# Two vectors held in PSUM, eight product tiles in a ring of six banks, and a new order in the first group

## The chip, the cores and the metric

The kernel runs on one core of one Trainium2 chip. The metric is the device time of one execution in microseconds (us). Engines are named as the profile names them: PE multiplies matrices (PEld is its weight load), DVE, ACT and POOL work element by element, SP only issues transfers. ACT and POOL issue transfers too; ACTq, SPq and POOLq are these queues.

## The reference, cut to what matters

Two graph layers, each with a residual and a layer norm, over 4096 nodes with 512 features. The change lies in the first layer, at its beginning:

```python
support = (inputs @ weight).reshape(N, H, D).transpose(1, 0, 2)       # N=4096, H=4, D=128
f1 = jnp.einsum('hnd,hdo->hn', support, weight_u)[:, None, :]
f2 = jnp.einsum('hnd,hdo->hn', support, weight_v)[:, :, None]
logits = f1 + f2
w = jnp.where(logits >= 0, logits, SLOPE * logits)
masked = w * adjacency[None]
mask = masked != 0
attn = jax.nn.softmax(jnp.where(mask, masked, NEG), axis=-1) * mask
out = jnp.einsum('hij,hjd->hid', attn, support)
out = out.transpose(1, 0, 2).reshape(N, H * D) + bias + inputs @ proj_w + proj_b
x = _layernorm(x + out)
```

The second layer is a masked attention with eight heads over the same adjacency, then a projection, a residual and a layer norm. All is float32. The change doesn't touch it.

## The kernel before, in words

**Stages.** The first stage computes x @ weight ("s", the support), x @ proj_w + x + biases ("b", the base) and the two dots of every support row and head with weight_u and weight_v. Then comes the first layer's aggregation: 4 windows of 1024 rows x 4 heads x 32 tiles of 128 nodes. After it come the second layer's projections and its attention.

**The first stage's groups.** The nodes are taken in eight groups of 512 (the loop over `g`, L900). A group multiplies its 512 x 512 block of x by two 512 x 512 weights, each by a scheme of seven products of half-size blocks in place of eight (Strassen-like, with sums of blocks of x and of the weights made beforehand). So a group has 14 products: numbers 1 to 7 for "s" and for "b"; the text writes s1, b1, s5 and so on. `product` (L831) does one: 4 float32 matmuls (the profile has 8 records for them), and then what follows on the other engines. Products 1, 5, 6 and 7 open a PSUM tile. Product 2 accumulates into the tile of 1, 3 into that of 5, 4 into that of 7, each after the first content has been read.

**What follows a product.** Products 1 and 5 are copied out by ACT (L862) and 2 too (L864). Product 6 is added by DVE (L866). Product 7 is added by DVE (L868), and POOL adds a further term (L870). Products 3 and 4 are added by DVE (L873); for b, POOL then adds the biases (L877) and SP stores the base (L879).

**The dots.** `dots(g, s4, n, m)` (L807) does 8 of the 32 dots of a group for a quarter of the support block: a DVE multiplication of a 128x128 slice of the support with a slice of `uv`, with a sum along the row (L813). `uv` (L644) holds both vectors on all partitions in SBUF. A dictionary `todo` (L903) says after which product each quarter is done. `factors` (L677), one group later, makes exponentials on ACT, scales the support on POOL (L696) and stores it.

**x.** `load_x` loads a group's x from SP, `turn_x` transposes it on DVE (four pieces a group, L736), and `combine_x` makes the four sums: 0 and 1 on DVE (L793, L795), 2 and 3 on POOL (L797, L800). Both run a group ahead.

**Weights.** The two weights come in column halves m and row halves c, in pieces of 64 KB: half 0 on ACT's queue, half 1 on SP's (`load_w0`, L657). `combine_w` (L759) makes sums of weight blocks: those of s on DVE, those of b on POOL. Before that POOL adds the identity into proj_w, 32 x 32 at a time (L889).

**PSUM.** Of the eight banks six form the ring `op` (tiles "o_ps"), in which a new tile waits until the one six before it has been read. The pool `xp` (tiles "x_ps") has the other two. Before the change products 7 live in `xp`; later in the kernel `xp` serves to transpose the first layer's result.

**Order.** The order of instructions on each engine is the order of the program text: nothing rearranges it. `Later` (L32 on) only puts calls off by a number of steps. The lambdas in `beside` (L718 on) put other work beside the products of given groups: the narrowing of the adjacency to bfloat16 (POOL's queue), its transposition (SP's queue), its shrinking to fp8 (ACT, L601), and in the last group the first three steps of the aggregation's front (`front`, L621: a sign on ACT, L628; a mask on DVE, L632; a weighting on DVE, L637). The aggregation's matmuls are L1055; they use tiles of the ring `op`.

## Time and profile before

| what | value |
|---|---|
| median of 3 runs | 3367.14 us (3366.89 to 3367.37) |
| the profiled execution's own time | 3365.75 us |
| its span, first to last instruction | 3364.0 us |
| PE busy | 3325.7 us (99% of the span) |
| DVE busy | 2423.3 us (72%) |
| POOL busy | 2227.4 us (66%) |
| ACT busy | 1986.5 us (59%) |
| 256 dots (L813) | 125.1 us on DVE, 549 ns mean |
| first product's start, first matmul of the aggregation | 7.66 us, 215.69 us |

A line of the timeline reads: start in us from the span's beginning, length in us, engine, line of the kernel, operation, output <- inputs with their shapes, count; in brackets how long the engine had been idle and what released it. Lengths of PE instructions are modelled, their starts are recorded, so distances between starts are used. A line of the page's list of groups reads: line, engine, operation, names and shapes, count | busy us, mean ns of one | idle time before, and what ended it.

### The profile page before, as it was taken

To read this page: it belongs to the slowest core of one execution; us is meant where nothing else is said; L and a number is where in the kernel's file an instruction comes from. 1 tells how busy PE (TensorE), PEld (TensorE's weight loads), DVE (VectorE), ACT (ScalarE), POOL (GpSimd) and SP (SyncE) were. 2 spreads that over 40 slices of the span, in tenths; PEclk is the share of its full clock that TensorE was granted. 3 is DMA by queue.
4 is the path that set the end of the run, shared out by engine and by line. 5 is a ranking of instruction groups with operands and counts; after the bars stand their busy time and mean duration, and the time that the engine had idled before them with its cause. 6 is when DMAs were issued, how large, how long until landed. Compare 5 with 4: busy or idle time off the path is not lost.

```text
span 3364.0 us, 66621 instructions
## 1 busy us (share of the span) xinstructions
PE 3325.7 (99%) x27050; PEld 1950.4 (58%) x27050; DVE 2423.3 (72%) x2892; ACT 1986.5 (59%) x2461; POOL 2227.4 (66%) x1590
## 2 busy tenths in 40 slices
PE   8999999999999999999999999999999999999998
PEld 7889999999999855643333333333333333333333
DVE  7999998898998711167776667666676766667676
ACT  1257877878876421156655656566566656656554
POOL 5641030040030365579999999999999999999996
PEclk9999999999999999999999999999999999999999
DMA  7968869679441443378889888989988889798884
GB/s 167 228 165 172 219 171 214 148 180 199 142 121 64 112 152 113 140 205 205 200 204 220 223 209 190 212 196 241 211 189 212 191 207 252 186 210 191 208 197 111
DMA packets 400335, 620.41 MB, mean 184 GB/s; under 512 B 166929, under 2 KB 249873, under 8 KB 398993
## 3 DMA queue, kind: packets, MB, share of 16 engines
q0 software_dynamic: 97520, 258.77, 42.1%
q1 hardware_dynamic: 300544, 354.92, 34.5%
q8 instruction: 215, 3.52, 0.4%
q10 hardware_dynamic: 1952, 2.36, 0.3%
q14 instruction: 104, 0.84, 0.1%
HBM read 315.87 MB, written 117.64 MB: 129 GB/s over the span
## 4 chain that ended last, share of the span: by engine, by line
PE 86%; DVE 6%; POOL 3%; DMA 3%; issue 1%; ACT 0%; SPq 0%; ACTq 0%; POOLq 0%; DVEq 0%
PE o_ps L1055 26%; PE o_ps L1368 24%; PE s_ps L1106 23%; PE s_ps L1171 5%; DVE prod L813 3%; PE s_ps L1432 3%; PE s_ps L1164 3%; POOL q_sum L1343 2%; DMA p<-p 2%; PE o_ps L845 1%; POOL p L1353 1%; PE s_ps L1387 1%; DVE p L637 0%; PE x_ps L1036 0%; DVE xT L736 0%
## 5 line engine op out<-in xcount | busy, mean ns | idle before, releaser
L1343 POOL TENSOR_TENSOR q_sum<-q_sum,p 128x1024 f32<-128x1024 f32 x538 | 1374.5, 2555 | 66.6 <-DMA p<-p 37.1
L1323 DVE TENSOR_TENSOR p<-s_ps,adjT 128x1024 f32<-128x1024 f32 x896 | 1044.8, 1216 | 467.6 <-ACT s_ps L1320 428.1
L1320 ACT ACTIVATE s_ps<-s_ps 128x1024 f32<-128x1024 f32 x1021 | 967.2, 1007 | 598.1 <-PE s_ps L1106 595.5
L1106 PE MATMUL s_ps<-q_sb,k_sb 64*64 64x512 f32 x8192 | 943.5, 589 | 3.0 <-DVE p L1323 3.0
L1368 PE MATMUL o_ps<-p,v_sb 64*64 64x512 f32 x8192 | 943.6, 590 | 0.0
L1055 PE MATMUL o_ps<-sup_t,p 128*128 128x129 f32 x8192 | 922.5, 275 | 4.6 <-DVE p L637 4.5
L1055 PEld LDWEIGHTS o_ps<-sup_t,p 128*128 128x128 f32 x8192 | 919.9, 192 | 5.3 <-DVE p L637 5.2
L637 DVE SCALAR_TENSOR_TENSOR p<-fr_t,dj,az 128x1024 f32<-128x1024 f32 x512 | 656.0, 1291 | 79.4 <-PE o_ps L1055 52.0
L1106 PEld LDWEIGHTS s_ps<-q_sb,k_sb 64*64 64x64 f32 x8192 | 312.2, 133 | 570.3 <-issue 451.5
L1368 PEld LDWEIGHTS o_ps<-p,v_sb 64*64 64x64 f32 x8192 | 310.3, 133 | 570.6 <-issue 560.6
L628 ACT ACTIVATE z<-fr_t,f 128x1024 fp8e4<-128x1024 f32 x512 | 558.3, 1145 | 119.2 <-DVE az L632 118.8
L1353 POOL DMA_DIRECT2D p<-p x412 | 438.0, 1302 | 10.2 <-PE o_ps L1368 8.6
L1019 POOL DMA_DIRECT2D agg<-base_d x32 | 28.7, 1206 | 516.0 <-ACT agg L1005 515.8
L1323 DVE TENSOR_TENSOR p<-s_ps,md 128x1024 f32<-128x1024 f32 x128 | 150.9, 1217 | 68.3 <-ACT s_ps L1320 62.1
L632 DVE TENSOR_TENSOR az<-adjT,z 128x512 int32<-128x512 int32 x256 | 175.6, 686 | 4.0 <-ACT z L628 3.4
L588 POOL COPY seen<-token 128x1 f32<-128x1 f32 x24 | 14.5, 606 | 245.9 <-DVE token L586 245.9
L1178 ACT ACTIVATE sb<-s_ps 128x1024 f32<-128x1024 f32 x35 | 35.8, 1023 | 191.9 <-PE s_ps L1171 129.1
L601 ACT ACTIVATE adjT<-stage 128x1024 fp8e4<-128x1024 bf16 x128 | 130.6, 1051 | 6.4 <-DMA stage<-adj_d 6.4
L1193 POOL TENSOR_TENSOR sb<-sb,sb 128x1024 f32<-128x1024 f32 x36 | 84.9, 2374 | 72.1 <-ACT sb L1178 72.1
L813 DVE CUSTOM_DVE_ANT_0 prod<-s,uv 128x128 f32<-128x128 f32 x256 | 125.1, 549 | 5.1 <-DMA uv<-in_L_gnn_weight_u_dram 2.6
L1217 DVE COPY k_sb<-s_ps 128x1024 f32<-128x1024 f32 x12 | 14.7, 1225 | 140.7 <-PE s_ps L1171 91.0
L1432 PE MATMUL s_ps<-wo_sb,on 128*128 128x512 f32 x240 | 110.8, 604 | 0.0
(187 smaller groups left out, 2176.5 us busy)
## 6 DMA issues: line engine op xcount, KB each, us to landing
p<-p POOLq DMA_DIRECT2D x412, 512.0 KB, 9.1
k_sb<-k_d SPq DMA_DIRECT2D x128, 512.0 KB
v_sb<-v_d SPq DMA_DIRECT2D x128, 512.0 KB
adj_d<-in_adj_dram POOLq DMA_DIRECT2D x32, 1024.0 KB, 10.9
sup_t<-sup_d SPq DMA_DIRECT2D x120, 258.0 KB
fr_t<-fr_d SPq DMA_DIRECT2D x16, 1024.0 KB
adjT_d<-adjT SPq DMA_DIRECT2D x32, 512.0 KB
adjT<-adjT_d SPq DMA_DIRECT2D x32, 512.0 KB
```

Of the source, the lines that this page charges most:

```text
L628: nc.scalar.activation(z[:, k, :], fr[:, 0, :], AF.Sign, bias=fs[j // GT][:, 0, (j + k) % GT, h:h + 1], saturate=False)
L632: nc.vector.tensor_tensor(az.bitcast(I32), adjT[w, j // CJ][:, j % CJ:j % CJ + 2, :].bitcast(I32), z.bitcast(I32), op=ALU.bitwise_and)
L637: nc.vector.scalar_tensor_tensor(p, fr[:, 1, :], dj[j // GT][:, j % GT, h:h + 1], az_t[w, h, j // 2][:, j % 2, :], op0=ALU.max, op1=ALU.mult)
L813: nc.vector.tensor_tensor_reduce(prod, s4[:, h, t, 0:D0], uv[:, k, h * D0:(h + 1) * D0], 1.0, 0.0, op0=ALU.mult, op1=ALU.add, accum_out=fs ...
L1055: nc.tensor.matmul(o[t // BK][:, t % BK, :], p[:, t * P:(t + 1) * P], s, start=(j == 0 and t % BK == 0), stop=(j == NT - 1), skip_group_ch ...
L1106: nc.tensor.matmul(s[c:c + MS, e, :], k[r, a + c:a + c + MS], qt[g, m][r, :], start=True, stop=True)
L1320: nc.scalar.activation(s, s, AF.Exp)
L1323: nc.vector.tensor_tensor(p, s, keep[:, None, :].to_broadcast([P, HP, G]), op=ALU.mult)
L1343: nc.gpsimd.tensor_tensor(q, q, p, op=ALU.add)
L1353: later.at(2, lambda: nc.gpsimd.dma_start(a, b, accum_op=ALU.add))
L1368: nc.tensor.matmul(o[c, n, :], v[r, j % CH, c], p[r, e, :], start=(j == 0), stop=(j == NT - 1))
L1432: nc.tensor.matmul(s, on_t[g][:, m, t * P:(t + 1) * P], wo_sb[:, m, :], start=(m == 0), stop=(m == NP1 - 1))
```

## The change

It has four parts. First, `uv` is copied by ACT into two PSUM tiles of `xp` before the first group, and the dots read these. Second, products 7 take their tiles from the ring `op`, so that eight tiles a group pass through six banks. Third, the first group has an order of its own for the 14 products (`begin`); the dots are placed by product rather than by position (in the later groups at the same places as before), and the first group's `turn_x` and `combine_x` for the next group come later. Fourth, on SP's queue the second half of weight comes ahead of the second half of proj_w, and POOL adds the identity to that half of proj_w after the sums of x; the weights' sums are regrouped.

```diff
-            for m, queue in ((0, nc.scalar), (1, nc.sync)):
+            for queue, m, srcs in ((nc.scalar, 0, ((w_sb, weight), (pw_sb, proj_w))),
+                                   (nc.sync, 1, ((w_sb, weight),)),
+                                   (nc.sync, 1, ((pw_sb, proj_w),))):
                 for c in range(2):
-                    for dst, src in ((w_sb, weight), (pw_sb, proj_w)):
+                    for dst, src in srcs:
                         load_w0(queue, dst, src, c, m)
...
-                                prod, s4[:, h, t, 0:D0], uv[:, k, h * D0:(h + 1) * D0], 1.0, 0.0,
+                                prod, s4[:, h, t, 0:D0], uv_ps[k][:, h, :], 1.0, 0.0,
...
-                if i in (1, 5, 6):
+                if i in (1, 5, 6, 7):
                     tiles[kind, i] = op.tile([P, G], F32, name="o_ps")
-                elif i == 7:
-                    tiles[kind, i] = xp.tile([P, GT, P], F32, name="x_ps").rearrange(
-                        "p t r -> p (t r)")
...
-            for m in range(2):
+            def add_identity(m):
...
+            add_identity(0)
             combine_x(0, 0)
             combine_w(nc.vector, "s", (5,))
-            combine_x(0, 1)
+            for i in (1, 2, 3):
+                combine_x(0, i)
             combine_w(nc.vector, "s", (6, 7, 4))
-            combine_w(nc.gpsimd, "b", (5, 6))
-            combine_x(0, 2)
-            combine_w(nc.gpsimd, "b", (7, 4))
-            combine_x(0, 3)
+            add_identity(1)
+            combine_w(nc.gpsimd, "b", (5, 6, 7, 4))
             nc.gpsimd.dma_start(bb, on_all_partitions(proj_b, D), accum_op=ALU.add)
-            kinds = ("s", "b")
+            uv_ps = [xp.tile([P, H0, D0], F32, name="x_ps") for _ in range(2)]
+            for k in range(2):
+                nc.scalar.activation(uv_ps[k], uv[:, k, :].rearrange("p (h d) -> p h d", h=H0),
+                                     AF.Copy)
+            usual = [(kind, i) for i in (1, 5, 2, 6, 7, 3, 4) for kind in ("s", "b")]
+            begin = [("s", 1), ("b", 1), ("s", 2), ("b", 2), ("s", 5), ("s", 6), ("s", 7),
+                     ("b", 5), ("s", 3), ("b", 6), ("s", 4), ("b", 7), ("b", 3), ("b", 4)]
             for g in range(NG):
...
-                todo = {5: lambda: dots(g, s4, 0, 0), 10: lambda: dots(g, s4, 0, 1),
-                        11: lambda: dots(g, s4, 1, 1), 12: lambda: dots(g, s4, 1, 0)}
-                plan = (1, 5, 2, 6, 7, 3, 4) if g else (1, 2, 5, 6, 7, 3, 4)
-                for k, (i, kind) in enumerate((i, kind) for i in plan for kind in kinds):
+                plan = usual if g else begin
+                todo = {}
+                for i, wait, n, m in ((2, 1, 0, 0), (3, 0, 0, 1), (7, 3, 1, 1), (4, 0, 1, 0)):
+                    todo.setdefault(plan.index(("s", i)) + wait, []).append((n, m))
+                for k, (kind, i) in enumerate(plan):
...
-                    if k in todo:
-                        todo[k]()
-                    first = 0 if g else 7
+                    for nm in todo.get(k, ()):
+                        dots(g, s4, *nm)
+                    first = 0 if g else 10
                     if g + 1 < NG and first <= k < first + KC:
                         turn_x(g + 1, k - first)
-                    first = 6 if g else 10
-                    if g + 1 < NG and first <= k < first + 4:
-                        combine_x(g + 1, k - first)
+                    if g + 1 < NG and (6 <= k < 10 if g else k == 13):
+                        for n in (k - 6,) if g else range(4):
+                            combine_x(g + 1, n)
```

## The prediction

> **What bounds the kernel now.** Measurement can tell about 0.2% (6.7 us) of this kernel from no change. The page says PE is busy 99% of the span, so only time in which PE waits can be won, and any new PE wait is paid. The change lies in the first stage (0 to about 226 us), so I read PE there in order of time: eight groups of 14 products, 8 matmul records each.

> ```profile
> 17.18 1.89 PE L845 MATMUL o_ps<-fr_t,p 128*128 128x256 f32 x8
> 23.26 5.26 PE L845 MATMUL o_ps<-fr_t,p 128*128 128x256 f32 x16 [4.20 <-POOL fr_t L759]
> 28.36 1.89 PE L845 MATMUL o_ps<-more_w,p 128*128 128x256 f32 x8
> 40.45 1.89 PE L845 MATMUL o_ps<-w_sb,xT 128*128 128x256 f32 x8
> 64.62 1.89 PE L845 MATMUL o_ps<-w_sb,xT 128*128 128x256 f32 x8
> ...
> 185.91 1.89 PE L845 MATMUL o_ps<-w_sb,xT 128*128 128x256 f32 x8
> ...
> 210.44 3.53 PE L845 MATMUL x_ps<-fr_t,xT 128*128 128x256 f32 x8 [3.65 <-DVE s L868]
> 215.69 5.52 PE L1055 MATMUL o_ps<-sup_t,p 128*128 128x129 f32 x48
> 225.53 26.30 PE L1055 MATMUL o_ps<-sup_t,p 128*128 128x129 f32 x208 [4.32 <-DVE p L637]
> ```

> Group 1 starts at 40.45, group 2 at 64.62: 24.17 us, which is 14 products of 1.727. PE is packed there. From group 1 to group 7 (185.91) it takes 145.46 us for 6 x 24.178 = 145.07: only 0.4 us is lost in the steady part. PE loses 4.2 us in group 0 and 3.65 + 4.32 us at the end, each followed by about 1.6 us of slow matmuls (two products from 23.26 take 5.10 us, not 3.45). At the end PE waits for DVE. Next, DVE and POOL there:

> ```profile
> 182.82 0.68 DVE L873 TENSOR_TENSOR s<-o_ps,z 128x512 f32<-128x512 f32 x1
> 189.20 0.28 DVE L813 CUSTOM_DVE_ANT_0 prod<-s,uv 128x128 f32<-128x128 f32 x1
> 189.41 2.44 DVE L813 CUSTOM_DVE_ANT_0 prod<-s,uv 128x128 f32<-128x128 f32 x1
> ```
> ```profile
> 182.38 1.09 POOL L870 TENSOR_TENSOR s<-s,z 128x512 f32<-128x512 f32 x1 [3.76 <-DVE s L868]
> 189.20 2.49 POOL L877 TENSOR_TENSOR base<-base,bb 128x1024 f32<-128x1024 f32 x1 [1.24 <-ACT y_sb L862]
> ```

> A dot alone takes 0.28 us and the next starts 0.21 later; the one that meets L877 takes 2.44, until POOL is done. L873, whose one input is in PSUM, runs its usual 0.68 us under POOL's L870. The 256 dots average 0.549 us. Last, the beginning, where the vectors arrive:

> ```profile
> 23.45 1.25 DVE L813 CUSTOM_DVE_ANT_0 prod<-s,uv 128x128 f32<-128x128 f32 x1 [2.60 <-DMA uv<-in_L_gnn_weight_u_dram]
> 26.04 1.16 DVE L813 CUSTOM_DVE_ANT_0 prod<-s,uv 128x128 f32<-128x128 f32 x1 [1.32 <-DMA uv<-in_L_gnn_weight_v_dram]
> ```

> The second vector lands at 26.04 us; today only dots wait for it.

> [...] ACT's small L681 at 221.12 waits for dots and L628 stands behind it. [...] The trace shows 0.50 at 24 to 26 and at 227 to 231 us.

> **The change, part by part.** Start, group 0. The two new ACT copies (vectors to PSUM) are written before every product, so they head ACT's queue. Each has the size of L862 (0.60 us). They replace no work, and the vectors' loads keep their place on SP, behind the same eight x loads and sixteen weight loads, so I take 26.04 again. Behind them on ACT stand the copies of s1, b1 and s2. Product s2 accumulates into s1's bank and must wait for s1's copy: today that copy ends at 13.22 and s2 starts at 13.72. New: the second copy ends at 26.64, s1's at 27.1, s2 starts at about 27.4, with only s1 and b1 done. Then 1.65 us of slow clock and 12 products x 1.727 = 20.72 give 49.8.

> The rest of the reordering hides under this wait. On SP the later half of proj_w goes behind that of weight: its last landing stays near 20.3, weight's comes about 2.6 us earlier. POOL then adds the second identity half (about 0.3 us an operation) until about 22 and makes b's four sums by 27 (4 x 1.26); b5, now eighth product, needs them at 37.7. DVE has the s sums by 20. Without the ACT wait POOL's b5 (about 23.2) would be PE's wait, 1 us or so: that is rival 2. The first adjacency copy stands behind the s7 addition on POOL, some 4 us later, and its reader comes two groups later.

> DVE in group 0: s3's result at 41.4 (L873 follows its matmul start by 2.0 us), then in queue order L873 0.72, eight dots 1.70, L866 0.60, eight dots 1.70, L873 0.72, eight dots 1.70, a transpose 0.60, L868 for b7 0.73: 49.9. Product b4 accumulates behind that L868, so it starts at 49.9 instead of 48.0: 1.9 us more. Group 1 starts at **51.7**, against 40.45: +11.2. Group 1's transposes are done by 50.4 for s1, and its x sum for s5 by 53.9, due 55.1.

> The ring of six. A tile now waits for the one six before. The tightest: b1 needs the DVE read of b3 (L873) of the group before. Today that read ends at 189.07, while b1 starts at 187.64. With dots at 0.21 it comes about 182.4 plus 0.7, 4 us before its need: nothing. If dots stayed slow it costs 1.4 us a group.

> Steady groups. Six groups x 24.178: group 7 starts at 196.7, 0.4 us won. DVE needs about 16 us of 24 (32 dots x 0.21 and some 9.3 of others), so it no longer drifts behind; its saved 9 us a group hide behind PE and win nothing.

> End. Today the chain from group 7's start to the end of the fourth weighting (L637, 225.47, for which PE waits) is 39.56 us. New, from 196.7: ACT's s2 and b2 copies, two shrinks and the first two signs (L628) end 15.1 later; L632 0.79, two L637 2.40, L632 0.72, one L637 1.20 to 20.2; L866, two L868 at 0.60 each, 22.0; L873 and eight dots 2.4; L873 and eight 2.3; L873 and eight 2.4; L873 0.6, two reductions and a transpose 0.3: 30.1. Then L637 meets POOL's L877 as today and takes 3.3: 33.4 us. That is 6.1 us won: dots 3.2, the rest because DVE meets group 7 without backlog. PE's own wait there falls from 3.65 to about 0.8 us[...]. The fourth weighting ends at 230.1 against 225.47. POOL's scaling and the adjacency transposes on SP start from the same point, so they move with it, and everything later is PE-bound and shifts.

> Two ends of what the trace doesn't show, a dot with a PSUM input: L866 (PSUM) and L759 (SBUF) both start 0.60 apart, so 0 extra[...]. I take 0, since the trace shows the pair. A gain below 0 is excluded by the 0.21 spacing, already the lone dot's.

> Sum: +11.2 - 0.4 - 6.1 = **+4.7 us**. The profiled execution, 3365.75 us (span 3364.0), becomes 3370.4; the median of runs is 1.4 higher, so **3371.8**.

> **The rivals.** 1, slower: the dot from PSUM is longer. 24 dots stand before b4 in group 0 and 24 before the fourth weighting; [...] from 42 ns each (2.0 us) it passes the 0.2%. [...] against: L866's 0.60. 2, faster: the ACT copies do not hold s1's copy (the vectors land by 12 us, or the copies are queued later). Then b5 at 23.2 is the limit, seven products follow, group 1 starts near 37 with the same b4 wait, some 14 us sooner: 3357. For it: the reordering works as meant; against: SP's loads and ACT's order. 3, the change doesn't do what it says: dots still wait for POOL. No gain at the end, +11.2, and up to 6 x 1.4 from the ring: 3378 to 3387. L873 under L870 speaks against it.

> **How the numbers follow.** Forecast 0.60 (its own range 3369 to 3375); rival 1 0.12; rival 2 0.10; rival 3 0.08; other mixtures 0.10, between. The range 3366 to 3379 leaves out rival 2 and most of rival 3. Faster by over 0.2%: rival 2 and a little, 0.12. Slower: 0.09 of the forecast's upper edge, 0.09 of rival 1, rival 3 and 0.04: 0.30. Within: 0.58.

> **What would show it.** Two ACT copies ending near 26.6 with s2 on PE near 27.4; b4 waiting for L868; group 1 near 51.7; groups 24.18 apart; dots of 0.28 us under POOL; the fourth weighting near 230. It is wrong if uv lands at another time, if a dot from PSUM takes over 0.3 us, or if PE waits for a ring tile.

## The result, and the profile after

The changed kernel takes 3375.88 us (median of 14 runs, 3373.32 to 3378.82), the kernel before 3367.26 us (14 runs, 3365.60 to 3373.02): a ratio of 1.0023 with a 95% interval of 1.0015 to 1.0031. Measured again later it took 3373.20 us, ratio 1.0019 (1.0011 to 1.0026). It is slower by about 0.2%. The forecast was 3371.8 us (+4.7) with a range of 3366 to 3379; the time lies in the range, some 4 us above the forecast in the first comparison and 1.4 us above it in the second.

The profiled execution took 3375.75 us (span 3374.0, 10.0 more than before). First PE's timeline of the changed kernel; the lines answer to those shown of the kernel before (L844 is the product's matmul, L1062 the aggregation's).

```profile
7.72 3.78 PE L844 MATMUL o_ps<-w_sb,xT 128*128 128x256 f32 x8 [7.72 <-DVE xT L738]
11.29 1.98 PE L844 MATMUL o_ps<-pw_sb,xT 128*128 128x256 f32 x8
28.00 3.78 PE L844 MATMUL o_ps<-w_sb,xT 128*128 128x256 f32 x8 [14.73 <-ACT z L861]
...
33.48 3.62 PE L844 MATMUL o_ps<-fr_t,p 128*128 128x256 f32 x16
...
45.57 3.62 PE L844 MATMUL o_ps<-pw_sb,p 128*128 128x256 f32 x16
50.87 1.97 PE L844 MATMUL o_ps<-more_w,xT 128*128 128x256 f32 x8 [1.69 <-DVE base L867]
52.67 1.89 PE L844 MATMUL o_ps<-w_sb,xT 128*128 128x256 f32 x8
...
197.71 1.89 PE L844 MATMUL o_ps<-w_sb,xT 128*128 128x256 f32 x8
...
219.38 1.99 PE L844 MATMUL o_ps<-fr_t,xT 128*128 128x256 f32 x8 [0.78 <-DVE s L867]
222.93 5.52 PE L1062 MATMUL o_ps<-sup_t,p 128*128 128x129 f32 x48
231.36 2.05 PE L1062 MATMUL o_ps<-sup_t,p 128*128 128x129 f32 x16 [2.90 <-DVE p L637]
```

After s1 and b1 PE stands idle for 14.73 us, and what ends this is ACT's copy of s1. Product b4 (50.87) waits 1.69 us for DVE. Group 1 starts at 52.67, 12.2 us later than before; group 7 at 197.71, 145.04 us after that, so nothing is lost in the steady groups. PE's wait ahead of s4 in the last group fell from 3.65 to 0.78 us, and the aggregation's fourth step starts at 231.36, 5.8 us later than before. ACT's timeline shows what held it:

```profile
23.93 0.60 ACT L901 ACTIVATE x_ps<-uv 128x512 f32<-128x512 f32 x1 [11.24 <-DMA uv<-in_L_gnn_weight_u_dram]
26.83 0.60 ACT L901 ACTIVATE x_ps<-uv 128x512 f32<-128x512 f32 x1 [2.29 <-DMA uv<-in_L_gnn_weight_v_dram]
27.36 0.58 ACT L861 ACTIVATE z<-o_ps 128x512 f32<-128x512 f32 x1
```

The two new copies wait for the vectors' loads, and the copy of s1 (L861) stands behind them. The dots themselves are as fast as hoped. The groups of the list, the kernel before first, the changed one second:

```profile
L813 DVE CUSTOM_DVE_ANT_0 prod<-s,uv 128x128 f32<-128x128 f32 x256 | 125.1, 549 | 5.1 <-DMA uv<-in_L_gnn_weight_u_dram 2.6 <-DMA uv<-in_L_gnn_weight_v_dram 1.3 <-ACT s L864 0.6
```
```profile
L815 DVE CUSTOM_DVE_ANT_0 prod<-s,x_ps 128x128 f32<-128x128 f32 x256 | 55.8, 283 | 41.0 <-ACT s L863 40.4
```

A dot's mean falls from 549 to 283 ns, and the longest of the 256 from 2.46 to 0.29 us. That a dot no longer waits for POOL is seen where both run at once, on POOL and on DVE:

```profile
195.96 2.36 POOL L876 TENSOR_TENSOR base<-base,bb 128x1024 f32<-128x1024 f32 x1 [0.40 <-issue]
```
```profile
195.94 0.28 DVE L815 CUSTOM_DVE_ANT_0 prod<-s,x_ps 128x128 f32<-128x128 f32 x1
196.15 0.28 DVE L815 CUSTOM_DVE_ANT_0 prod<-s,x_ps 128x128 f32<-128x128 f32 x1
196.36 0.28 DVE L815 CUSTOM_DVE_ANT_0 prod<-s,x_ps 128x128 f32<-128x128 f32 x1
```

DVE's time thus won is spent waiting for ACT's copies (40.4 us of idle time before the dots), since PE sets the pace.

### The profile page after: what moved, and what is told of

It is laid out like the page before. It is cut to its first block, busy times and chain, and to the rows that moved or that the text cites. A ratio compares the mean times of both kernels' runs of the same rounds, so it can differ in the third digit from the quotient of the medians.

```text
span 3374.0 us, 66618 instructions
## 1 busy us (share of the span) xinstructions
PE 3321.3 (98%) x27050; PEld 1946.6 (58%) x27050; DVE 2362.1 (70%) x2892; ACT 1987.5 (59%) x2463; POOL 2227.8 (66%) x1590
## 4 chain that ended last, share of the span: by engine, by line
PE 92%; DMA 3%; POOL 2%; DVE 2%; issue 1%; ACT 1%; SPq 0%; ACTq 0%; POOLq 0%; DVEq 0%
PE o_ps L1062 26%; PE o_ps L1375 24%; PE s_ps L1113 24%; PE s_ps L1178 5%; PE o_ps L844 5%; PE s_ps L1439 3%; PE s_ps L1171 3%; DMA p<-p 2%; POOL q_sum L1350 1%; PE s_ps L1394 1%; DVE p L637 0%; PE x_ps L1043 0%; POOL p L1360 0%; DMA stage<-adj_d 0%; DMA k_d<-v_sb 0%
## 5 line engine op out<-in xcount | busy, mean ns | idle before, releaser
L1062 PE MATMUL o_ps<-sup_t,p 128*128 128x129 f32 x8192 | 920.5, 275 | 6.2 <-DVE p L637 6.1
L1062 PEld LDWEIGHTS o_ps<-sup_t,p 128*128 128x128 f32 x8192 | 917.3, 192 | 7.3 <-DVE p L637 7.2
L637 DVE SCALAR_TENSOR_TENSOR p<-fr_t,dj,az 128x1024 f32<-128x1024 f32 x512 | 656.0, 1291 | 78.6 <-PE o_ps L1062 51.4
L628 ACT ACTIVATE z<-fr_t,f 128x1024 fp8e4<-128x1024 f32 x512 | 558.0, 1144 | 117.5 <-DVE az L632 117.2
L632 DVE TENSOR_TENSOR az<-adjT,z 128x512 int32<-128x512 int32 x256 | 175.7, 686 | 7.5 <-ACT z L628 6.8
L588 POOL COPY seen<-token 128x1 f32<-128x1 f32 x24 | 14.0, 582 | 245.9 <-DVE token L586 245.9
L1409 ACT ACTIVATE r<-r_h 32x256 f32<-32x256 f32 x248 | 102.3, 412 | 2.9
```

What stands on the lines that cost most here:

```text
L628: nc.scalar.activation(z[:, k, :], fr[:, 0, :], AF.Sign, bias=fs[j // GT][:, 0, (j + k) % GT, h:h + 1], saturate=False)
L632: nc.vector.tensor_tensor(az.bitcast(I32), adjT[w, j // CJ][:, j % CJ:j % CJ + 2, :].bitcast(I32), z.bitcast(I32), op=ALU.bitwise_and)
L637: nc.vector.scalar_tensor_tensor(p, fr[:, 1, :], dj[j // GT][:, j % GT, h:h + 1], az_t[w, h, j // 2][:, j % 2, :], op0=ALU.max, op1=ALU.mult)
L1062: nc.tensor.matmul(o[t // BK][:, t % BK, :], p[:, t * P:(t + 1) * P], s, start=(j == 0 and t % BK == 0), stop=(j == NT - 1), skip_group_ch ...
```

## The experiments

The theory: the copies at the head of ACT's queue tie the second product to the landing of the vectors (A). The rivals: the new order itself costs the time, the ring of six costs, or reading from PSUM is worth nothing. Ten runs were made, on three occasions. The table has all of them: when the second vector landed (the start of the first instruction that waits for it), the starts of s2, of group 1 and of the aggregation's fourth step on PE, the start of POOL's first L588 (a marker some 35 us after that step), the median, and the ratio to the kernel before on the same chip and occasion with its interval. The first five columns come from one profile each. The kernel before had a median of 3368.15 us beside e1, e2, e3 and e5, 3368.30 beside e4, e7, e8 and e9, and 3369.34 beside e6 and e10; so ratios compare across occasions, medians do not. A ratio is not quite the quotient of two medians. All times are in us.

| kernel | landing | s2 | group 1 | 4th step | marker | median | ratio |
|---|---|---|---|---|---|---|---|
| before | 26.04 | 13.72 | 40.45 | 225.53 | 260.41 | 3367.26 | 1 |
| changed | 26.83 | 28.00 | 52.67 | 231.36 | 267.14 | 3375.88 | 1.0023 (1.0015 to 1.0031) |
| e1 copies later | 25.13 | 13.04 | 39.89 | 219.17 | 255.49 | 3363.97 | 0.9986 (0.9979 to 0.9993) |
| e2 order alone | 25.66 | 13.16 | 42.39 | 226.11 | 262.22 | 3370.47 | 1.0001 (0.9992 to 1.0010) |
| e3 PSUM and ring, old order | 25.73 | 26.90 | 50.22 | 228.90 | 265.15 | 3371.27 | 1.0008 (1.0001 to 1.0015) |
| e4 ring alone | 25.97 | 13.88 | 40.71 | 225.77 | 261.87 | 3368.43 | 1.0001 (0.9992 to 1.0009) |
| e5 vectors earlier | 20.84 | 22.01 | 46.48 | 225.16 | 261.65 | 3370.28 | 1.0006 (0.9999 to 1.0013) |
| e6 vectors later | 29.54 | 30.71 | 56.13 | 234.82 | 271.14 | 3377.91 | 1.0027 (1.0016 to 1.0039) |
| e7 as e1, last dots at the end | 26.14 | 13.21 | 38.12 | 216.65 | 253.25 | 3361.04 | 0.9975 (0.9967 to 0.9983) |
| e8 changed, dots from SBUF | 25.70 | 26.87 | 51.80 | 234.28 | 270.70 | 3379.44 | 1.0034 (1.0024 to 1.0045) |
| e9 as e7, vectors earlier, s3 and s4 earlier | 20.48 | 12.88 | 35.99 | 214.51 | 251.29 | 3361.15 | 0.9975 (0.9963 to 0.9987) |
| e10 changed again | 25.94 | 27.11 | 51.88 | 230.55 | 266.48 | 3373.20 | 1.0019 (1.0011 to 1.0026) |

**e1: the copies behind s5's copy.** The edit on the changed kernel:

```diff
-            for k in range(2):
-                nc.scalar.activation(uv_ps[k], uv[:, k, :]..., AF.Copy)
...
-                for i, wait, n, m in ((2, 1, 0, 0), ...
+                for i, wait, n, m in ((2, 1 if g else 2, 0, 0), ...
...
                     product(g, s4, kind, i)
+                    if g == 0 and k == 4:
+                        for n in range(2):
+                            nc.scalar.activation(uv_ps[n], uv[:, n, :]..., AF.Copy)
```

> The changed kernel with one thing moved: the two ACT copies of the vectors stand behind the copy of product s5 in the first group, and the first eight dots behind product s5. Theory A (the copies at the head of ACT's queue hold PE for the vectors' load): s2 starts near 13.7 us instead of 28.0, the dots then wait for the vectors to about 27.4 and hold DVE, so product s4 starts near 31 and b4 near 39.5, group 1 near 41 instead of 52.7, and the time falls by about 11.4 us to 3364.5. Theory B (the new order of products and loads costs the time, the copies do not): s2 may start earlier but group 1 stays within 3 us of 52.7 and the time at 3373 or more.

Measured: 3363.97 us, below both kernels. PE in the first group:

```profile
13.04 1.99 PE L844 MATMUL o_ps<-w_sb,xT 128*128 128x256 f32 x8 [0.21 <-ACT z L861]
...
23.41 1.99 PE L844 MATMUL o_ps<-fr_t,p 128*128 128x256 f32 x8 [1.38 <-POOL fr_t L761]
...
37.10 3.00 PE L844 MATMUL o_ps<-more_w,xT 128*128 128x256 f32 x8 [2.89 <-DVE base L867]
39.89 2.59 PE L844 MATMUL o_ps<-w_sb,xT 128*128 128x256 f32 x8
```

The 14.73 us of waiting are gone, and group 1 starts 12.8 us sooner. Two more waits come out, both small: b5 for POOL's sum of weights, and b4 for DVE's addition of b7. The place of two ACT instructions, and with them of the first eight dots, which read what they write, decides the sign of the whole change.

**e5 and e6: the vectors' loads moved on SP's queue.** e5 puts them ahead of the second half of proj_w, e6 behind `load_x(1)`:

```diff
# e5
                                    (nc.sync, 1, ((pw_sb, proj_w),))):
+                if srcs[0][0] is pw_sb:
+                    nc.sync.dma_start(uv[:, 0, :], on_all_partitions(weight_u, D))
+                    nc.sync.dma_start(uv[:, 1, :], on_all_partitions(weight_v, D))
...
# e6
+            load_x(1)
             nc.sync.dma_start(uv[:, 0, :], on_all_partitions(weight_u, D))
             nc.sync.dma_start(uv[:, 1, :], on_all_partitions(weight_v, D))
-            load_x(1)
```

> The changed kernel with the two vectors' loads on SP's queue put ahead of the second half of proj_w (eight loads earlier). Theory A: PE's wait in the first group follows the landing of the second vector one for one: issue about 4.5 us earlier, landing near 22.3 instead of 26.8, s2 near 23.5 instead of 28.0, group 1 near 48.1, time about 3371.3; the later half of proj_w lands some 2 us later, which POOL's sums (needed at about 33) still cover. Theory B: no change beyond 1 us.

> The changed kernel with the two vectors' loads on SP's queue put behind the eight loads of x for group 1. Theory A (PE waits for the second vector one for one): issue some 10 us later, landing near 37, s2 near 38.3, group 1 near 63, time about 3386. Theory B (the wait is partly covered by something else that is late anyway): less than half of that, 3380 or below.

PE's two lines in e5, then in e6:

```profile
22.01 3.71 PE L845 MATMUL o_ps<-w_sb,xT 128*128 128x256 f32 x8 [8.58 <-ACT z L862]
...
46.48 1.89 PE L845 MATMUL o_ps<-w_sb,xT 128*128 128x256 f32 x8
```
```profile
30.71 3.78 PE L844 MATMUL o_ps<-w_sb,xT 128*128 128x256 f32 x8 [17.06 <-ACT z L861]
...
56.13 1.89 PE L844 MATMUL o_ps<-w_sb,xT 128*128 128x256 f32 x8
```

In all six profiles with the copies at the head (changed, e3, e5, e6, e8, e10) s2 starts 1.17 us after the landing, at landings from 20.84 to 29.54 us, and among the five of them with the new order group 1 follows 25.6 to 26.6 us after the landing. That is one for one but for PE's slow start after the wait: s2 and b2 took 5.27 us in e5 (22.01 to 27.28) and 6.24 us in e6 (30.71 to 36.95), against 3.45 at full speed, and this is the 1 us between the two. The sizes were missed. In e5 the vectors landed 1.5 us sooner than expected. In e6, `load_x(1)` is four transfers and not eight, so the issue moved by 2.0 us (21.37 against 19.42 in e10) and the landing by 3.6, not by 10. The time of e6 alone, 3377.91, would have spoken for Theory B (3380 or below); what decides for A is the 1.17 us. Against e10 the markers of e5 and e6 move by -4.8 and +4.7 us. The median of e6 moves by +4.7 as well; e5 was run on another occasion, and its ratio lies 0.0013 below that of e10, some 4 us.

**e10: the changed kernel again.**

> The changed kernel once more, as it is. Theory A (the landing of the second vector, 26.8 us in its first profile and 25.1 to 26.1 in five kernels with the loads in the same place, varies from one execution to the next): it lands between 25 and 27 us, s2 starts 1.2 us after it, group 1 starts 25.8 us after it, time 3375 plus or minus 2. Theory B (the new order of loads makes it late): again 26.8.

The second vector landed at 25.94 and not at 26.83, with the loads in the same order; in e1 it was 25.13, in e8 25.70. The forecast's 26.04 was a fair value; the 26.83 of the first profile is scatter, about half of it in SP's issue of the load (20.38 against 19.89 us).

**e3: PSUM and ring with the old order; e2: the new order alone.** e3 is the kernel before with the tiles of product 7 in `op`, the copies at the head, and dots from `uv_ps`. e2 is the changed kernel without the copies, with dots from `uv` and product 7 in `xp`.

> The kernel before with only the vectors in PSUM (copies at the head of ACT's queue) and products 7 in the ring of six; order and loads of the first group as before. Theory A: s2 waits for the copies to 27.2 to 28, then 2.0 us of slow clock and 12 products of 1.727 give group 1 near 50.2, without the wait of b4 for DVE that the new order has; the end wins 6 us as in the changed kernel: about 3373.4, 2.5 us below the changed kernel. Theory B: without the new order the kernel is at 3367 or below.

> The kernel before with only the new order in the first group and the new order of loads: dots read the vectors in SBUF, products 7 keep their two banks of their own. Theory A: no ACT wait, so s2 starts near 13.7; the dots hold DVE until the vectors land (about 27), group 1 starts near 42.5 against 40.45 before; the steady groups and the end are as before (dots meet POOL), so about +2 us: 3369. Theory B: the order is the loss: group 1 near 50, and 3374 or more.

e3 took 3371.27 us, about 3 us more than the kernel before beside it (1.0008): the kernel is still not faster. Group 1 starts at 50.22, 24.5 us after the landing and not 25.6 to 26.6, so in the first group the copies cost less without the new order than with it. No b4 wait shows, as the old order has DVE's addition of b7 four products ahead of b4. e2 took 3370.47 us, 1.0001, which leaves open whether it differs at all; in its profile group 1 starts 1.9 us later than before, as expected.

**e4: the ring alone.** The only edit on the kernel before:

```diff
-                if i in (1, 5, 6):
+                if i in (1, 5, 6, 7):
                     tiles[kind, i] = op.tile([P, G], F32, name="o_ps")
-                elif i == 7:
-                    tiles[kind, i] = xp.tile([P, GT, P], F32, name="x_ps").rearrange(
-                        "p t r -> p (t r)")
```

> The kernel before with products 7 in the ring of six and nothing else: dots still read the vectors in SBUF and wait for POOL. Theory A (the ring is free only while the dots are fast): product b1 of each later group waits for the read of b3 of the group before, which today ends about 1.4 us after b1 should start; six or seven groups give up to 8 to 10 us, 3375 to 3378, with a wait of PE at b1 in the later groups. Theory B (the ring costs nothing in any case): 3367, no such wait.

Theory A was wrong. The ratio is 1.0001, and the read that b1 was to wait for ends after b1 has started. PE's b1 of group 7, then DVE's read of b3 of group 6:

```profile
187.88 1.89 PE L842 MATMUL o_ps<-pw_sb,xT 128*128 128x256 f32 x8
```
```profile
188.63 0.68 DVE L870 TENSOR_TENSOR base<-o_ps,az 128x512 f32<-128x512 f32 x1
```

So b1 does not take the bank of b3's tile, the one six before. The rule that a new tile waits for the one six before, as told ahead of the prediction, does not hold here; which bank it takes instead was not looked into. No cost of the ring shows, even with slow dots.

**e8: the changed kernel with dots from SBUF.** Nobody reads the copies, which stay.

```diff
-                                prod, s4[:, h, t, 0:D0], uv_ps[k][:, h, :], 1.0, 0.0,
+                                prod, s4[:, h, t, 0:D0], uv[:, k, h * D0:(h + 1) * D0], 1.0, 0.0,
```

> The changed kernel with the dots reading the vectors in SBUF as before; the copies to PSUM stay where they are and nobody reads them. Theory A: dots again wait for POOL (mean near 0.5 us instead of 0.28), the end gives back its 6 us, and b1 waits in the ring as above: 3382 to 3390. Theory B (reading from PSUM is worth nothing): 3376 and dots of 0.28 us also here.

It took 3379.44 us (1.0034). The dots are slow again, as Theory A has it, but the time is below its 3382 to 3390: the ring costs nothing, and the end gives back less than 6 us. The list of groups and the fourth step of the aggregation:

```profile
L815 DVE CUSTOM_DVE_ANT_0 prod<-s,uv 128x128 f32<-128x128 f32 x256 | 108.0, 483 | 15.8 <-ACT s L863 15.2
```
```profile
234.28 26.30 PE L1062 MATMUL o_ps<-sup_t,p 128*128 128x129 f32 x208 [6.02 <-DVE p L637]
```

From group 7's start (196.84) to the fourth step it takes 37.4 us, against 33.65 in the changed kernel and 39.6 in the kernel before. So reading from PSUM is worth 3.8 us at the end once the new first group is there. In e3, with the old first group, the same stretch is 33.6 us (195.26 to 228.90), so there PSUM gives all 6 us. With dots from SBUF and the new first group (e8, and e2 with 188.66 to 226.11) 37.4 us remain: 2.2 us come with the new order alone. The two overlap. The traces show where the 2.2 us lie: in DVE's arrears at the start of group 7. DVE reads b4 of group 6 9.35 us after group 7's start in the kernel before, 7.17 us after it in e2 and e8, and 2.08 us after it in the changed kernel and e3. In the new order PE has waited for DVE at the first group's b4, so that at group 1's start this lag was 0.2 us in e2 and e8 and 7.4 us in the kernel before. No run tested it.

**e7 and e9: a version that beats both.** e7 takes e1 and moves the first group's last eight dots to the group's end; e9 adds e5's order of loads and puts s3 and s4 ahead of b5.

```diff
# e7, on e1
+                                      (4, 0 if g else 9, 1, 0)):
...
                             combine_x(g + 1, n)
+                    if not g and k == 13:
+                        dots(g, s4, 1, 0)
...
# e9, on e7 and e5's loads
-                     ("b", 5), ("s", 3), ("b", 6), ("s", 4), ("b", 7), ("b", 3), ("b", 4)]
+                     ("s", 3), ("s", 4), ("b", 5), ("b", 6), ("b", 7), ("b", 3), ("b", 4)]
...
+                for i, wait, n, m in ((2, 1 if g else 5, 0, 0), (3, 0, 0, 1),
+                                      (7, 3 if g else 4, 1, 1), (4, 0 if g else 9, 1, 0)):
```

> As the kernel whose copies stand behind s5's copy, and in the first group the last eight dots go to the group's end, behind the sums of x. Theory A (b4's wait is for DVE, whose queue holds eight dots ahead of b7's addition): that wait of 2.9 us and the slow clock after it go, group 1 starts near 37.5 instead of 39.9, time about 3361.7. Theory B (b4 waits for something else): group 1 stays near 39.9 and the time at 3364.

> As the kernel with the last dots at the end, and besides: the vectors' loads ahead of the second half of proj_w, and products s3 and s4 ahead of b5. Theory A: the vectors land near 21, PE has no wait for POOL's sums before b5 (25.3), group 1 starts near 34 to 35.5, time about 3358 to 3359.5, below both kernels. Theory B (something else limits the first group, the load of x for group 1 say): group 1 not before 37, time 3362 or more.

PE's b4 and the start of group 1 in e7, then in e9:

```profile
36.32 1.97 PE L844 MATMUL o_ps<-more_w,xT 128*128 128x256 f32 x8 [1.09 <-DVE base L867]
38.12 1.89 PE L844 MATMUL o_ps<-w_sb,xT 128*128 128x256 f32 x8
```
```profile
34.19 1.97 PE L845 MATMUL o_ps<-more_w,xT 128*128 128x256 f32 x8 [1.86 <-DVE base L868]
35.99 1.89 PE L845 MATMUL o_ps<-w_sb,xT 128*128 128x256 f32 x8
```

Both are faster than the kernel before by 0.25% (0.9975), 3361.04 and 3361.15 us; so the change's parts can win, and the place of the copies took away more than that. e7 came out as expected. e9 missed its 34 to 35.5 and 3358 to 3359.5: group 1 starts at 35.99, 2.1 us before e7's, and its marker is 2.0 us earlier, but the medians don't tell the two apart. In the profiles the lead shrinks to 0.7 us by the end of the first layer's aggregation (its last matmul starts at 1141.3 against 1142.0); in e9 PE waited 2.08 us at 242.90 and its next 156 matmul records took 19.32 us, 124 ns each, in e7 it waited 1.81 us at 244.86 and the next 149 took 17.30 us, 116 ns each, which could account for it. In both, b4 still waits for DVE, for 1.1 and 1.9 us.

## Why the prediction was right or wrong

**Right, the mechanism.** Step by step in the first profile after: s2 at 28.00 (forecast 27.4), b4 at 50.87 after a wait for L867 (49.9), group 1 at 52.67 (51.7), 24.17 us a group (24.178), the stretch at the end 33.65 us (33.4), dots of 0.28 us under POOL. e1, which takes the wait away, and e5 and e6, which move it, show that the wait is the cause. In the second profile of the changed kernel, whose landing was near the assumed one, group 1 starts at 51.88 and the fourth step at 230.55, against 51.7 and 230.1.

**Right, the PSUM price.** Taking 0 for a PSUM input was right: dots start 0.21 us apart. Rival 1 falls. By the time alone it would not: from 42 ns a dot it stands at 3373.8 or more, which the first median, 3375.88, is past, and that median lies 0.9 us above the forecast's own range of 3369 to 3375, with the second, 3373.20, inside it. A slowing by over 0.2%, which came in the first comparison and not quite in the second (1.0019), had been given 0.30.

**Missed sizes.** Start: +12.2 us and not +11.2, of which 0.8 is the landing and 0.4 the slow clock (28.00 to 33.48 is 5.48 us for two products, 2.03 more than at full speed, forecast 1.65), less small change. Steady groups -0.4 and end -6.0, as forecast; that the wait ahead of s4 would cost no clock was the author's estimate, and after its 0.78 us the clock stayed at 1.00. That gives the +5.8 at the fourth step (+5.0 in e10). From there the forecast let everything shift alike. SP issues the adjacency transposes 5.84 us later than before, but ACT, which waits for the first, goes on 6.75 later, at 252.51 against 245.76, and the marker is 6.7 us later (267.14 against 260.41; in e10 6.1). This is not shown to be the change's doing. From SP's issue to ACT's going on it takes 9.97 us in the profile before and 10.9 to 11.9 us in the eleven others, e4 among them (11.20), whose code there is that of the kernel before. So it is that one profile which was short; against e4's marker the changed kernel is 5.3 us later, and e10 4.6.

**The remaining 2 of 8.6 us** of the first comparison have no place in the first layer, where the shift stays at 6.7 us to the last L588. From the marker to the end of the span the code is the same in all twelve profiles, and that stretch takes 3101.8 us (e4) to 3110.2 us (e5), 3103.6 in the kernel before and 3106.9 in the changed one. This is scatter as far as the runs show; what causes it was not tested. By the intervals of the two comparisons the change costs between 4 and 10 us.

**Wrong, the ring.** The step that priced the ring at 1.4 us a group with slow dots, and with it most of rival 3's width, rested on a wait for the tile six before, and e4 shows none. The forecast itself had the ring at nothing, since the dots would be fast, so its sum was not touched: right in the number, by a reason that was not needed. e8's 3379.44 lies within rival 3's 3378 to 3387 only since the end gives back 3.8 us.

**Rival 2, the faster case,** was priced at 3357 with copies that hold nothing. e1, which makes it so, came to 3364 and not 3357. Its b5 is where the rival had it (23.41, priced at 23.2), but group 1 starts at 39.89 and not near 37. The rival missed that DVE's first dots wait for the vectors and hold DVE's additions behind them, so that b4 waits until 37.10 and then takes 3.00 us, at a clock of 0.50 from 37.9 us. DVE in e1:

```profile
23.40 0.29 DVE L815 CUSTOM_DVE_ANT_0 prod<-s,x_ps 128x128 f32<-128x128 f32 x1 [3.33 <-ACT x_ps L920]
...
25.76 0.29 DVE L815 CUSTOM_DVE_ANT_0 prod<-s,x_ps 128x128 f32<-128x128 f32 x1 [2.07 <-ACT x_ps L920]
```

## What to carry to other kernels

In the changed kernel two ACT copies of 0.60 us that waited for loads until 26.83 us held the copy of s1 behind them, and with it PE for 14.73 us; queued behind s5's copy they held neither (e1: s2 at 13.04). So a small preparation should be written where its operand has landed, not where it can first be named. Taking the dots' waits for POOL off DVE, which isn't the bound here, won only where DVE's lateness reached PE: the dots lost 69 of their 125 us, and what that won was 6 us, at the end of the stage.

## What the runs showed of the hardware that was not expected

The record of the clock in the traces shows what differs. In the profiles of the kernel before and of the changed one, each stretch between two changes of the clock is a whole number of steps of 3.413 us: 3.413 twice, 6.827, 10.240, 184.320 and 3123.195 us before, 13.653 and 3331.408 us after. So the time can be taken in steps of that length that end at the changes. The question is how an idle time falls into them:

| run | step, us | share of it in which PE was busy | clock after it |
|---|---|---|---|
| e1 | 34.47 to 37.88 | 0.23 | 0.50 |
| before | 207.33 to 210.74 | 0.09 | 0.50 |
| before | 220.98 to 224.39 | 0.07 | 0.50 |
| changed | 226.49 to 229.90 | 0.58 | 1.00 |
| changed | 229.90 to 233.32 | 0.57 | 1.00 |

Over the profiles of the kernel before and of the changed one, each of the 6 steps after which the full clock was halved had PE busy for at most 0.09 of it (by the modelled lengths of PE's instructions), and each of the more than 1900 after which it stayed full for at least 0.48. With e1's 0.23, the step's share separates the cases seen here, and the length of the idle time does not: of two gaps of 2.9 us one was followed by the slow clock and the other was not.
